# Layer 1 in the order of every fourth token, layer-0 entries turned by DMA, and a work list with shorter latencies: a four-layer graph network on one core

## The chip, the cores and the metric

The kernel runs on one core of a Trainium2 chip. The core has five engines with a queue each: TensorE (PE, matmul; its weight loads are shown as PEld), VectorE (DVE), ScalarE (ACT), GpSimd (POOL) and SyncE (SP), which here only issues DMAs. Each engine takes its instructions strictly in the order in which they stand in its queue and waits on semaphores for what the others produce. The metric is the device time of one execution in microseconds (us). Before the change it is 1746.38 us, the median of three runs (1745.01 to 1746.55).

## The reference

A batch of 32 graphs of 512 tokens with 128 features goes through four layers that share one adjacency matrix of zeros and ones. Each layer adds its result to x, after a layer norm and a relu:

```python
h = jnp.maximum(_layernorm(x, axis=-1), 0.0)
x = x + layer(h, adj, ...)
```

Layer 0 is an attention-like layer: `x_h = elu(h @ Wi + bi)`, two scores per token from `We`, `e = sigmoid(a_tgt[:, :, None] + a_src[:, None, :] + be)` times a mask made from the adjacency, then `agg = e @ x_h`, `self_part = x_h * sum(e, axis=-1)`, and two more products (`Wn` with an elu, `Wm`). Layer 1 is a gated recurrent unit of five steps:

```python
m_in = m_out = jnp.einsum('nm,bmd->bnd', adj, h)
av = jnp.concatenate([m_in, m_out], axis=-1)
u3 = h @ u3_w.T + u3_b
z = sigmoid(av @ w3_w.T + w3_b + u3); r = sigmoid(av @ w4_w.T + w4_b + u3)
hv = tanh(av @ w5_w.T + w5_b + (r * h @ u5_w.T + u5_b))
h = (1.0 - z) * h + z * hv
```

Layer 2 is `adj @ (h @ weight) + bias`. Layer 3 is a sum over powers zero to three of the adjacency, each with its own weight.

## The kernel before

A graph's tensor is one tile of 128 partitions by 512 f32 (256 KB). It is held in one of two ways: tokens on partitions (four chunks of 128 tokens side by side), or turned, with the features on partitions and 512 tokens along the row. Work goes in groups of four graphs (`G = 4`), eight groups. The tokens-on-partitions form is what the adjacency products take as the stationary operand, and what layer norm and the final sums need; the gate products need the turned form.

The kernel does not write its instructions in the order of the mathematics. It first lists operations: `op(engine, us, due, emit, reads, writes, ...)` records an engine, a duration, a due time and the values read and written. `Plan.order` (line 98) then plays the list through: at each moment it gives each engine that is free the ready operation with the earliest due time, provided that buffers are free (`slots`, line 223: 36 of kind f in SBUF, 8 PSUM banks of kind b, and so on). An operation's result counts as known `result` us after its end: the class constant `RESULT` (line 45) or a value of its own for DMAs. The outcome fixes the order of every engine's queue. Durations and due times are numbers written in the code; they change nothing but this order.

`begin(b)` (line 560) sets the due time of graph b: 14 us apart for the first ones (`FIRST_PACE`, line 217), 56 us apart later (`PACE`), so that at any time several graphs are in flight in different layers.

An adjacency entry that TensorE's fast f32r format cannot hold would need an exact f32 path. The kernel counts such entries (L424, L431, L436), branches once (L812 and L813, with everything up to a planned 30 us before the branch) and runs one of two lists. With zeros and ones it is the list with `A_r`, the f32r adjacency, where a token operand is split into a high and a low f32r part (`parts`, L672 on ScalarE and L675 on VectorE) and each adjacency product is eight passes (L686). The f32 products with the weights are all made by `product` (L357); each shows in the profile as two instructions.

- **Layer 0, entry.** `copied(transposed(h))`: four 128x128 transposes on TensorE (L329) into PSUM, a ScalarE copy (L352), then the product with Wi.
- **Layer 0, scores.** L469 makes messages and two scores per token; L476 puts the scores into `ends`, one column per chunk. One score is needed as a row on all partitions. For the first four graphs TensorE spreads it (`spread`, L493). For the others `gather` (L488) writes the four columns to DRAM as a row of 512 elements, and a second DMA (L502) reads it back to all 128 partitions.
- **Layer 0, sums.** GpSimd adds the four tiles of e (L516, three additions per graph) and one product with ones sums over partitions (L357 `ones` for the first four graphs; L533, L534 and L539 in f32r for the others).
- **Layer 1.** Its first turned h comes from TensorE like layer 0's. A step has the products u3, adjacency, w4, w3, w5 and u5, two VectorE additions (L704), three tanh (L362) and four more VectorE operations (L711, L721, L723, L725). Then `turned` (L337) brings the new h back to tokens on partitions without TensorE: VectorE transposes 32x32 blocks, reading every fourth token of a row, a DMA writes the result to DRAM (L340, m<-f) and a second one reads it back in pieces of 512 bytes, rearranged (L342, f<-m).
- **Layers 2 and 3.** L743; and L760 with L769.

SP issues all DMAs in one queue. A DMA that reads what another wrote waits in that queue until the other has landed.

Of the kernel before, what the change touches and what calls it, by code (L numbers as in the profile page):

```python
# [11 lines left out]
F32R = mybir.dt.float32r  # L12
# [4 lines left out]
P = 128  # L17
# [21 lines left out]
class Plan:  # L39
# [5 lines left out]
    RESULT = {"PE": 0.5, "ACT": 0.5, "DVE": 0.5, "POOL": 0.6, "SP": 2.5}  # L45
# [51 lines left out]

    def order(self, end=None):
# [9 lines left out]
        for i, o in enumerate(left):  # L108
            index[o] = i
            o.waits = sum(not b.begun for b in o.before)  # L110
            o.ready = max([0.0, *(b.known for b in o.before if b.begun)])
            if not o.waits:
                heapq.heappush(coming[o.eng], (o.ready, i, o))
                events.append(o.ready)
# [16 lines left out]
        while events:  # L131
# [3 lines left out]
            for e in self.until:  # L135
# [33 lines left out]
                for a in o.after:  # L169
                    if a in index:  # L170
                        a.waits -= 1
                        a.ready = max(a.ready, o.known)
# [8 lines left out]
def tile_four_graph_layers(  # L181
# [30 lines left out]
    G = 4  # L212
# [4 lines left out]
    PACE, FIRST_PACE, LAST_PACE = 56.0, 14.0, 30.0  # L217
# [3 lines left out]
    T_VEC, T_COPY, T_ACT = 0.61, 0.5, 0.6  # L221

    slots = {"x": 6, "f": 36, "q": 4, "s": 8, "d": 4, "m": 8, "b": 8}
# [8 lines left out]
    def buffers(pool, kind, n, shape, dt=F32):  # L232
# [7 lines left out]
        "d": buffers(dram, "d", slots["d"], [1, N]),  # L240
# [92 lines left out]
    def turned(src, due):  # L333


        blocks, moved, t = Val("f"), Val("m"), Val("f")
        op("DVE", 1.03, due, lambda: nc.vector.transpose(  # L337
            at(blocks).rearrange("p (q c f) -> p q c f", c=NC, f=32),
            at(src).rearrange("p (c i q) -> p q c i", c=NC, q=4)), [src], [blocks])
        op("SP", 1.0, due, lambda: nc.sync.dma_start(at(moved), at(blocks)),  # L340
           [blocks], [moved], result=4.0)
        op("SP", 1.0, due, lambda: nc.sync.dma_start(  # L342
            at(t).rearrange("p (b e) -> p b e", e=P),
            at(moved).rearrange("(b i) (q e) -> (i q) b e", i=32, e=P)), [moved], [t], result=6.0)
# [10 lines left out]
    def product(w, src, due, dst=None, start=True, stop=True):  # L355
        dst = dst or Val("b")
        op("PE", T_MM, due, lambda: nc.tensor.matmul(  # L357
            at(dst), at(w), at(src), start=start, stop=stop), [src, w], [dst])
# [50 lines left out]
    A_r, mask = const("A_r", [P, NC, N], F32R), const("mask", [P, NC, N])  # L409
    inexact = const("inexact", [1, 1], I32)  # L410
    n_odd = const("n_odd", [P, NC])
    for jc in range(NC):
        pt, z, odd = Val("b"), Val("f"), Val("f")
        def turn(jc=jc, pt=pt):
# [9 lines left out]
        op("DVE", 0.7, jc, lambda jc=jc, pt=pt, odd=odd: nc.vector.scalar_tensor_tensor(  # L424
            at(odd), at(A_r)[:, jc, :].bitcast(F32), 1.0, at(pt),
            op0=ALU.mult, op1=ALU.not_equal, accum_out=at(n_odd)[:, jc : jc + 1]),
            [A_r, pt], [odd, n_odd])
    p_odd = Val("b")
# [6 lines left out]
    op("PE", 0.3, 8, count, [n_odd, ones], [p_odd])  # L435
    op("DVE", 0.2, 8, lambda: nc.vector.tensor_copy(at(inexact), at(p_odd)[:1, :1]),  # L436
# [18 lines left out]
    def layer0(b, h, due):  # L455
        KEEP = 12
        hT = copied(transposed(h, due), due)
        d = due + 6
        xhT = elu(product(Wi_sb, hT, d), bi_sb, bi_half, d, KEEP)
# [25 lines left out]
        row, tgt = Val("d"), Val("f")  # L485
        def gather():
            with nc.allow_non_contiguous_dma(reason="a column of chunks becomes a row"):
                nc.sync.dma_start(  # L488
                    at(row).rearrange("o (c p) -> p (o c)", c=NC), at(ends)[:, NC : 2 * NC]
                )  # L490
# [9 lines left out]
        else:  # L500
            op("SP", 0.6, due + 10, gather, [ends], [row], result=11.0)
            op("SP", 0.6, due + 14, lambda: nc.sync.dma_start(  # L502
                at(tgt), at(row).to_broadcast([P, N])), [row], [tgt], keep=KEEP, result=7.0)
        es = []
        for jc in range(NC):
            e = Val("f")
            op("ACT", T_ACT, d, lambda e=e, jc=jc: nc.scalar.activation(
                at(e), at(tgt), AF.Tanh, bias=at(ends)[:, jc : jc + 1]), [tgt, ends], [e],
# [5 lines left out]
        sums = [Val("f"), Val("f")]  # L514
        def add(dst, a, c):
            op("POOL", 1.4, d, lambda: nc.gpsimd.tensor_tensor(  # L516
                at(dst), at(a), at(c), op=ALU.add), [a, c], [dst])
# [334 lines left out]
```

## Time and profile before

| | |
|---|---|
| median of three runs | 1746.38 us |
| the profiled execution | 1748.12 us |
| its span, first to last instruction | 1746.3 us |
| mean granted TensorE clock | 0.994 |
| DMA: moved, mean share of 16 engines | 112 MB, 24% |

Some groups of instructions, by line and tile:

| line, engine | what | count | mean ns | busy us |
|---|---|---|---|---|
| L337 DVE | transpose of 32x32 blocks, layer 1 | 160 | 1105 | 176.5 |
| L704 DVE | addition of u to a gate | 320 | 679 | 213.6 |
| L510 DVE | (tanh + 1) times mask, layer 0 | 128 | 900 | 107.8 |
| L516 POOL | sums of e, layer 0 | 96 | 1608 | 154.1 |
| L352 ACT | copies of PSUM to SBUF | 448 | 588 | 256.5 |
| L329 PE | transposes with the identity | 384 | 277 | 57.6 |

A row of the profile's groups gives busy time and the mean duration of one. Durations of matmuls overlap (a transpose is shown as 277 ns, though four follow each other in 0.44 us), so TensorE's work is better counted from how far long runs reach in the chain of waits. VectorE's instructions overlap a little too: a 128x512 elementwise one is shown as about 680 ns, and the next begins 600 ns after it.

The busy time by stretch, in us:

| stretch | PE | DVE | ACT | POOL | clock |
|---|---|---|---|---|---|
| 0-50 | 28.92 | 33.52 | 32.91 | 23.33 | 0.93 |
| 50-250 | 196.41 | 186.66 | 144.94 | 57.03 | 1.00 |
| 250-1450 | 1179.32 | 1051.69 | 805.69 | 290.17 | 0.99 |
| 1450-1700 | 249.17 | 194.38 | 145.15 | 29.23 | 1.00 |
| 1700-1746.3 | 41.66 | 13.02 | 6.47 | 0.00 | 0.98 |

### The profile page before, as it was taken

The page shows a single profiled execution, that of the slowest core. Times are in us where ns is not written, and L with a number is a line of the kernel's source. Part 1 is how long each engine was busy: PE and PEld are TensorE (multiplying, and loading weights), DVE is VectorE, ACT ScalarE, POOL GpSimd, SP SyncE. Part 2 cuts the span into 40 slices and gives each one's busy share as a digit, 9 for nine tenths or more (in the row PEclk, how much of TensorE's full clock was granted, in tenths as well). Part 3 has the DMA queues.
Part 4 walks back from the last instruction along what each step waited for, and adds up shares of the span by engine and source line. Part 5 has one row for each costly group of instructions (what it writes and reads, how often), then busy time and mean ns, then how long its engine had stood idle before and what let it go on. Part 6 is the DMA issues. An engine that isn't in the chain of part 4 may idle for free.

```text
span 1746.3 us, 21006 instructions
## 1 busy us (share of the span) xinstructions
PE 1695.5 (97%) x6829; PEld 1098.0 (63%) x6829; DVE 1479.3 (85%) x3213; ACT 1135.2 (65%) x2155; POOL 399.8 (23%) x312
## 2 busy tenths in 40 slices
PE   5899999999999999999999999999999999999998
PEld 3555555566666666665666666666666656656797
DVE  6899999999898887888888898888899879878752
ACT  6767765778666666665765667666768656655451
POOL 4521210332222211222212221122232212001110
PEclk9999999999999999999999999999999999999999
DMA  4022322322222222223221221222322131221201
GB/s 109 7 53 75 85 73 73 81 52 85 52 58 61 79 67 46 74 75 55 67 55 60 79 61 61 67 52 81 67 67 55 50 84 61 73 72 58 76 13 48
DMA packets 164534, 112.07 MB, mean 64 GB/s; under 512 B 23232, under 2 KB 139840, under 8 KB 164416
## 3 DMA queue, kind: packets, MB, share of 16 engines
q1 hardware_dynamic: 164416, 110.65, 23.9%
q8 instruction: 55, 0.90, 0.3%
q14 instruction: 63, 0.52, 0.2%
HBM read 60.23 MB, written 50.39 MB: 63 GB/s over the span
## 4 chain that ended last, share of the span: by engine, by line
PE 76%; DVE 13%; DMA 4%; ACT 3%; issue 2%; SPq 0%; DVEq 0%; ACTq 0%
PE b L357 33%; PE b L686 17%; PE b L769 9%; PE b L760 6%; DMA f<-m 4%; PE b L525 4%; PE b L552 3%; DVE f L510 2%; PE b L329 2%; DVE f L704 2%; PE b L743 2%; PE b L469 1%; DVE f L337 1%; DVE f L723 1%; DVE r L675 1%
## 5 line engine op out<-in xcount | busy, mean ns | idle before, releaser
L686 PE MATMUL b<-A_r,r 128*128 128x512 f32 x1536 | 427.6, 421 | 4.3 <-DVE r L675 4.2
L352 ACT COPY f<-b 128x512 f32<-128x512 f32 x448 | 256.5, 588 | 210.6 <-PE b L686 119.2
L686 PEld LDWEIGHTS b<-A_r,r 128*128 128x128 f32 x1536 | 287.2, 189 | 109.6 <-issue 38.9
L391 POOL TENSOR_TENSOR s<-s,nhalf 128x4 f32<-128x4 f32 x128 | 156.2, 1221 | 735.9 <-DVE s L389 707.8
L769 PE MATMUL b<-r,A_r 128*128 128x512 f32 x768 | 306.3, 499 | 0.0
L704 DVE TENSOR_TENSOR f<-f,b 128x512 f32<-128x512 f32 x320 | 213.6, 679 | 56.5 <-PE b L357 54.0
L399 ACT ACTIVATE f<-x,s 128x128 f32<-128x128 f32 x512 | 209.9, 488 | 22.3 <-DVE s L394 22.2
L769 PEld LDWEIGHTS b<-r,A_r 128*128 128x128 f32 x768 | 140.6, 189 | 102.6 <-issue 91.5
L516 POOL TENSOR_TENSOR f<-f,f 128x512 f32<-128x512 f32 x96 | 154.1, 1608 | 207.4 <-DVE f L510 131.1
L362 ACT ACTIVATE f<-f,b4w 128x512 f32<-128x512 f32 x160 | 115.8, 724 | 127.3 <-DVE f L704 126.6
L337 DVE STREAM_TRANSPOSE f<-f 128x512 f32<-128x512 f32 x160 | 176.5, 1105 | 0.3
L675 DVE TENSOR_TENSOR r<-f,r 128x512 fp32r<-128x512 f32 x192 | 141.3, 739 | 37.1 <-ACT r L672 37.0
L357 PE MATMUL b<-f,u5T 128*128 128x512 f32 x320 | 163.2, 595 | 8.7 <-DVE f L711 8.7
L357 PE MATMUL b<-f,w4T 128*128 128x512 f32 x320 | 165.2, 599 | 4.1 <-ACT f L352 4.0
L357 PE MATMUL b<-f,w3T 128*128 128x512 f32 x320 | 163.8, 594 | 0.0
L357 PE MATMUL b<-f,w5T 128*128 128x512 f32 x320 | 163.2, 595 | 0.0
L357 PE MATMUL b<-f,u3T 128*128 128x512 f32 x320 | 162.7, 592 | 0.0
L721 DVE TENSOR_TENSOR f<-f,f 128x512 f32<-128x512 f32 x160 | 121.5, 761 | 39.3 <-ACT f L362 39.1
L760 PEld LDWEIGHTS b<-V,f 128*128 128x128 f32 x1024 | 131.7, 191 | 31.1 <-issue 25.1
L362 ACT ACTIVATE f<-b,b5w 128x512 f32<-128x512 f32 x160 | 109.7, 688 | 60.4 <-PE b L357 60.2
L362 ACT ACTIVATE f<-f,b3w 128x512 f32<-128x512 f32 x160 | 115.0, 721 | 50.8 <-DVE f L704 50.5
L525 PE MATMUL b<-f,f 128*128 128x512 f32 x256 | 130.9, 596 | 3.2 <-issue 3.0
(95 smaller groups left out, 2489.9 us busy)
## 6 DMA issues: line engine op xcount, KB each, us to landing
m<-f SPq DMA_DIRECT2D x160, 256.0 KB, 2.0
f<-m SPq DMA_DIRECT2D x160, 256.0 KB, 2.8
x<-in_x_dram SPq DMA_DIRECT2D x32, 256.0 KB, 4.5
out_dram<-x SPq DMA_DIRECT2D x32, 256.0 KB, 2.4
f<-d SPq DMA_DIRECT2D x28, 256.0 KB, 4.1
f<-in_adj_dram SPq DMA_DIRECT2D x4, 256.0 KB, 4.6
f<-in_L_gnn_weight_dram SPq DMA_DIRECT2D x2, 224.0 KB, 2.6
d<-s SPq DMA_DIRECT2D x28, 2.0 KB, 9.1
```

What stands on the lines that cost most here:

```text
L337: op("DVE", 1.03, due, lambda: nc.vector.transpose(at(blocks).rearrange("p (q c f) -> p q c f", c=NC, f=32), at(src).rearrange("p (c i q) ...
L352: op("ACT", us, due, lambda: nc.scalar.copy(at(t), at(src)), [src], [t])
L357: op("PE", T_MM, due, lambda: nc.tensor.matmul(at(dst), at(w), at(src), start=start, stop=stop), [src, w], [dst])
L362: op("ACT", us, due, lambda: nc.scalar.activation(at(dst), at(src), AF.Tanh, bias=at(bias), scale=scale), [src, bias], [dst])
L391: op("POOL", 1.2, due, lambda: nc.gpsimd.tensor_tensor(stat(SCALE), stat(VAR), at(neg_half), op=ALU.pow), [s, neg_half], [s])
L399: nc.scalar.activation(at(h)[:, ts(c, P)], at(X[b])[:, c, :], AF.Relu, bias=stat(SHIFT)[:, c : c + 1], scale=stat(SCALE)[:, c : c + 1],)
L525: op("PE", T_MM, d, lambda jc=jc: nc.tensor.matmul(at(pn), at(msg)[:, ts(jc, P)], at(es[jc]), start=jc == 0, stop=False), [msg, es[jc]], [pn])
L675: op("DVE", T_VEC, due, lambda: nc.vector.tensor_tensor(part(lo), whole(), part(hi).bitcast(F32), op=ALU.subtract), [src, hi], [lo], two=two)
L686: nc.tensor.matmul(at(pa), at(part)[:, ts(jc, P)], at(adjT)[:, jc, :], start=jc == n == 0, stop=jc == NC - 1 and n == PARTS - 1,)
L704: op("DVE", T_VEC, d, lambda: nc.vector.tensor_tensor(at(s), at(u), at(pg), op=ALU.add), [u, pg], [s])
L760: nc.tensor.matmul(at(pz)[:, ts(i, D)], at(hT[i])[:, ts(ic, P)], at(V[k]), start=i == 0, stop=last and i == G - 1,)
L769: nc.tensor.matmul(at(pz), at(adjT)[:, jc, ts(ic, P)], at(part), start=False, stop=jc == NC - 1 and n == PARTS - 1,)
```

## The change

- **Layer 1 runs with its turned tiles in another token order.** In a chunk of 128 tokens, the 32 tokens 0, 4, 8, ... come first, then 1, 5, 9, ..., and so on. The copy into the first turned h makes this order (line 753 of the changed kernel), and layer 1's adjacency products take their columns from `A_fours`, a copy of the adjacency with its columns in the same order, made once by four ScalarE copies. `turned` now reads 32 elements in a row per block.
- **Layer 0 of graphs 4 to 31 gets its turned h by DMA**: `turned_back`, the same three operations as `turned` in the other direction, in place of the TensorE transposes and the copy. Its columns come out in blocks; the product with Wi reads them through a view with four dimensions.
- **The row of scores** goes to DRAM as 128 rows of 128 bytes: a VectorE transpose `flip` of the score columns, each repeated eight times, then one DMA; the read back takes the four rows of each quarter that are needed. The tile stays in blocks, and the tanh reads it through a view.
- **The first four graphs' sums** of e are four products with ones on TensorE; GpSimd's additions remain for the others, later due.
- **The list**: smaller `RESULT` values, no or a smaller delay between operations of the same engine (`known`), 0.45 us per DMA issue, 2.6 and 3.6 us for DMA results, `FIRST_PACE` 10 instead of 14, layer 1 of the first four graphs due 0.75 instead of 1.2 paces after layer 0, the count of inexact entries due later, five x buffers instead of six, and one free r buffer kept by `parts`.

```diff
-    RESULT = {"PE": 0.5, "ACT": 0.5, "DVE": 0.5, "POOL": 0.6, "SP": 2.5}
+    RESULT = {"PE": 0.25, "ACT": 0.2, "DVE": 0.2, "POOL": 0.2, "SP": 2.5}
...
+    def known(self, o, to):
+
+        own = {"PE": 0.0, "ACT": 0.13, "DVE": 0.13}
+        return o.known - o.result + own[o.eng] if to.eng == o.eng in own else o.known
...
-                        a.ready = max(a.ready, o.known)
+                        a.ready = max(a.ready, self.known(o, a))
...
-    PACE, FIRST_PACE, LAST_PACE = 56.0, 14.0, 30.0
+    PACE, FIRST_PACE, LAST_PACE = 56.0, 10.0, 30.0
...
-    slots = {"x": 6, "f": 36, "q": 4, "s": 8, "d": 4, "m": 8, "b": 8}
+    slots = {"x": 5, "f": 36, "q": 4, "s": 8, "d": 4, "m": 8, "b": 8}
...
     def turned(src, due):
...
+        op("DVE", 0.63, due, lambda: nc.vector.transpose(
+            at(blocks).rearrange("p (q c f) -> p q c f", c=NC, f=32),
+            at(src).rearrange("p (c q i) -> p q c i", c=NC, q=4)), [src], [blocks])
+        op("SP", T_DMA, due, lambda: nc.sync.dma_start(at(moved), at(blocks)),
+           [blocks], [moved], result=2.6)
+        op("SP", T_DMA, due, lambda: nc.sync.dma_start(
+            at(t).rearrange("p (b e) -> p b e", e=P),
+            at(moved).rearrange("(b i) (q e) -> (i q) b e", i=32, e=P)), [moved], [t], result=3.6)
+        return t
+
+    def turned_back(src, due):
+
         blocks, moved, t = Val("f"), Val("m"), Val("f")
         op("DVE", 1.03, due, lambda: nc.vector.transpose(
-            at(blocks).rearrange("p (q c f) -> p q c f", c=NC, f=32),
-            at(src).rearrange("p (c i q) -> p q c i", c=NC, q=4)), [src], [blocks])
-        op("SP", 1.0, due, lambda: nc.sync.dma_start(at(moved), at(blocks)),
-           [blocks], [moved], result=4.0)
...
+            at(blocks).rearrange("p (b c i) -> p b c i", c=NC, i=32),
+            at(src).rearrange("p (c f b) -> p b c f", c=NC, b=4)), [src], [blocks])
...
+    for jc in range(NC):
+        op("ACT", 0.52, 30, lambda jc=jc: nc.scalar.copy(
+            at(A_fours)[:, jc, :].rearrange("p (c q i) -> p c q i", c=NC, q=4),
+            at(A_r)[:, jc, :].rearrange("p (c i q) -> p c q i", c=NC, q=4)), [A_r], [A_fours])
...
-        hT = copied(transposed(h, due), due)
+        if b < G:
+            hT = copied(transposed(h, due), due)
+        else:
+            hT = turned_back(h, due)
+            due += 6
         d = due + 6
-        xhT = elu(product(Wi_sb, hT, d), bi_sb, bi_half, d, KEEP)
+        xhT = elu(product(Wi_sb, hT, d, blocks=b >= G), bi_sb, bi_half, d, KEEP)
...
+        def turn():
+            nc.vector.transpose(
+                at(flip)[:, :32].rearrange("p (k c) -> p k c", c=NC),
+                at(ends)[:, None, NC : 2 * NC].to_broadcast([P, 32 // NC, NC]))
         def gather():
-            with nc.allow_non_contiguous_dma(reason="a column of chunks becomes a row"):
-                nc.sync.dma_start(
-                    at(row).rearrange("o (c p) -> p (o c)", c=NC), at(ends)[:, NC : 2 * NC]
-                )
+            nc.sync.dma_start(at(row), at(flip)[:, :32])
+        def read():
+            rows = at(row).rearrange("(q k) i -> q (k i)", k=32)[:, :P]
+            nc.sync.dma_start(
+                at(tgt).rearrange("p (q e) -> p q e", e=P), rows[None].to_broadcast([P, 4, P]))
...
         if b < G:
-            ps = product(ones, sums[0], d)
+            ps = Val("b")
+            for jc in range(NC):
+                product(ones, es[jc], d, ps, start=jc == 0, stop=jc == NC - 1)
         else:
...
-            h = copied(transposed(h, due), due)
+            pt, h = transposed(h, due), Val("f")
+            op("ACT", T_COPY, due, lambda h=h, pt=pt: nc.scalar.copy(
+                at(h).rearrange("p (c q i) -> p c q i", c=NC, q=4), at(pt).rearrange("p (c i q) -> p c q i", c=NC, q=4)), [pt], [h])
...
-                m = copied(times_adj(tok, d), d)
+                m = copied(times_adj(tok, d, fours=True), d)
...
-                t = begin(b) + (2.0 if G <= b < B - G - 1 else 1.2) * PACE
+                t = begin(b) + (0.75 if b < G else 2.0 if b < B - G - 1 else 1.2) * PACE
```

## The prediction

> **What bounds the kernel now.** I read the shares of busy time first, then the busy time by slice, then I counted TensorE's work, then looked for the places where TensorE stands.
>
> ```profile
> span 1746.3 us, 21006 instructions
> PE 1695.5 (97%) x6829; PEld 1098.0 (63%) x6829; DVE 1479.3 (85%) x3213; ACT 1135.2 (65%) x2155; POOL 399.8 (23%) x312
> ...
> PE   5899999999999999999999999999999999999998
> ```
>
> TensorE is busy nearly everywhere, but matmul ends are modelled, so 97% does not say how much could be saved. I therefore count. The chain of waits gives the pace of long runs:
>
> ```profile
> 1599.16 8.58 PE b L357 x20
> 1691.38 5.36 PE b L760 x48
> 941.19 0.44 PE b L329 x4
> ```
>
> That is 0.429 us for an f32 128x512 instruction (two make one product, 0.858), 0.112 for a 128-wide one, 0.11 for a transpose (four are 0.44). The same view has 1.85 us for eight adjacency passes of L686 (0.231) and 6.36 for 28 of L769 (0.227). Times the counts of the groups: 1992 f32 instructions (5 x 320 gate ones, 256 of L525, 64 + 64 + 8 of Wi, Wn, ones) 854.6; 1536 of L686 354.8; 768 of L769 and 56 of L539 187.9; 2048 narrow ones (L760, L552, L743, L469) 228.8; 421 transposes 46.3. Sum **1672 us**, so the span holds about 74 us in which TensorE has nothing to do or runs at a lower clock. Doing the same count in stretches, the loss is 27.7 us in 0-50 (22.6 of it before 30), 4.8 in 50-250, 33.0 in 250-1450, 1.6 in 1450-1700 and 4.6 in the tail. The change can take instructions off TensorE, or these losses.
>
> The middle's losses come in lumps; three 50-us stretches alone lose 4.4, 5.6 and 4.1. Around one of them, first SP's DMA issues in order of time, then the chain, then TensorE's instructions, then one window (its length, busy PE, PEld, DVE, ACT, POOL, the granted clock, DMA):
>
> ```profile
> 792.54 0.36 SPq L488 DMA_DIRECT2D d<-s  x1
> 793.07 0.39 SPq L342 DMA_DIRECT2D f<-m  x1
> ```
>
> ```profile
> 793.07 11.55 DMA f<-m
> ```
>
> ```profile
> 806.38 2.08 PE L357 MATMUL b<-f,w4T 128*128 128x512 f32 x2 [2.15 <-ACT f L352]
> ```
>
> ```profile
> 807.00:808.00 1.00, 1.00 (x2) 0.34 (x1) 0.32 (x1) 1.00 (x4) 0.00 (x0) 0.50 0.04 14
> ```
>
> A write d<-s (one column of scores) is issued, and the f<-m right behind it lands after 11.55 us instead of its usual 2.8. ScalarE's queue stands on it (L672), so VectorE's and TensorE's do: 2.15 us of nothing, and then a clock of 0.50. The chain shows six such f<-m (304, 356, 518, 687, 793, 1417 us), each right behind a d<-s; those of 304, 793 and 1417 reach TensorE and are the three lumps.
>
> ```profile
> m<-f SPq DMA_DIRECT2D x160, 256.0 KB, 2.0
> f<-m SPq DMA_DIRECT2D x160, 256.0 KB, 2.8
> ...
> d<-s SPq DMA_DIRECT2D x28, 2.0 KB, 9.1
> ```
>
> The 2 KB of d<-s go as 512 pieces of 4 bytes and take 9.1 us, longer than 256 KB in 128 rows.
>
> **The change, part by part.**
>
> *Entries of layer 0 (graphs 4 to 31).* Four transposes per graph leave TensorE: 28 x 0.44 = **-12.3 us** where it is the bound; a ScalarE copy of 0.59 each goes too (off the path, 65% busy). In their place stand a VectorE transpose with the stride of today's L337, which takes 1.02 us from issue to issue, and an m/f pair of DMAs: 1.02 + 2.0 + 2.8 plus two issues of 0.35, some 6.5 us, before Wi. The list gives 6 us more for it, and three or four graphs in flight stand on TensorE's queue meanwhile: cost nothing; uncovered, it would be up to 6.5 us a graph. A rule speaks against this edit: the Trainium skill (VectorE: DVE Perf Modes, "Rules for kernel authors") says to use TensorE for a 128x128 transpose if a PSUM destination is acceptable, and its "The three transpose paths" warns of plain DMAs with strides. By the rule the 12.3 us stay in the sum (1729 below). The rows say otherwise here: 512-byte pieces land in 2.8 us, and the engine that is relieved is the one that is full. I take the row. Wi then reads its operand in 128-byte runs; no row shows that, between 0 and a doubling (28 x 0.858 = 24 us); I take 0, as an f32 product takes 0.858 us for 512 columns and so reads slowly.
>
> *Rows of layer 0.* d<-s becomes a small VectorE transpose (0.1-0.2 us, like the 0.2 of L476) and a DMA of 128 rows of 128 bytes. Its landing lies between 2.0 (m<-f, also 128 rows) and 9.1 (the present one). By number of pieces it is nearest to m<-f, so I take about 2. Then an f<-m behind it has nothing to wait for. What a lump costs: the Trainium skill (TensorE: Matmul & The Clock Gate, "Why this matters for your kernels") puts the loss of clock at idle gaps over about 3 us; by that the three stalls cost their gaps alone, 3 x 2.1 = 6.3. Here gaps of 2.1 us are followed by some 3 us at 0.50, so the measured 4.4 + 5.6 + 4.1 = **-14.1 us** stands. f<-d (4.1) stays 256 KB, in 512-byte pieces.
>
> *Token order in layer 1.* L337 (160 times) reads 32 elements in a row instead of every fourth. Between today's 1.02 and the 0.60 of every elementwise 128x512 row I take 0.60: 160 x 0.42 = -67 us of VectorE, against +28 x 1.02 for the new transposes and 28 small ones (+4): -34 us, from 85% busy to 83%. In 50-250 it is 93% busy (186.66 of 200). A_fours costs four ScalarE copies, about 2.4 us once, off the path; L686's moving operand stays contiguous, so 0.231 stays. The 32 copies that reorder h read PSUM with a stride: 0.59 up to twice that, on ScalarE, hidden. The x slots go from 6 to 5: a group lives some 800 us of the list's 224 per group, under four slots.
>
> *First four graphs.* The three POOL adds per graph (1.3-1.8 us each, in series, L516) go and TensorE does four "ones" products instead of one: 12 x 0.858 = **+10.3 us**. In graph 0 the product of ones starts at 37.97 today although its L510 are done at 30.9. Together with the 12.3: TensorE's work falls by 2.0 to **1670**.
>
> *The head.* Before 30 us it waits for the adjacency (first matmul at 6.3), for VectorE (busy without a break from 9.8 to 20) and for 3 us of branch: the same instructions stand before the branch, so its 22 us stay. After it, in the order in which the changed kernel's instructions stand on each engine, TensorE has 28 us of work up to the first adjacency pass of layer 1 and VectorE 20 us, for which about 29 us are there (31 to 60); today the first pass comes at 73.7, and 30-60 lose 6.1 us. Layer 1, which asks 6.1 us of TensorE per step for 5 of VectorE, comes earlier (0.75 instead of 1.2 paces). I take 2 us of loss for 31-60 and 2 for 60-250 instead of 6.1 and 3.3, and 22 before: 26 for 32.5, **-6.5 us**. Ends: -9.5 (1 us lost after 31) and 0.
>
> *The list's latencies.* Results count as known after 0.2-0.25 us instead of 0.5, DMAs after 2.6 and 3.6 instead of 4 and 6 (medians 2.0 and 2.8). Nothing is added or removed; order changes. The remaining 33.0 - 14.1 = 18.9 us of the middle are waits for VectorE such as the one at 931 (L721 and L711 1.68 us each beside POOL's L516). Less VectorE work and later-due POOL adds shorten it; a tighter order has less slack. Bounds: all 18.9 gone, or 19 more. I take a third off, **-6 us**.
>
> Sum against the profiled 1746.3: -2.0 - 14.1 - 6.5 - 6 = **1717.7 us**. The profiled execution took 1748.1 in all, 1.7 over the median 1746.4, so a median of the runs near 1717.
>
> **Rivals.** *(1) The middle keeps its stalls.* The lumps at 310, 800 and 1430 go, but the tighter order opens others, since slack that covered VectorE's delays is gone. For it: VectorE is still 83% busy and in order; against it: three of the four clock losses have one cause. Only -2.0 and -6.5 remain, with up to a few us of the rest: 1737. *(2) The middle becomes clean:* all 33.0 go and the head gains 9.5: 1746.3 - 2 - 33 - 9.5 = 1702. *(3) Slower: SP's queue.* SP issues in order and stands at each f<-m until its m<-f has landed (272.5 us in all, 124 waits). 28 more pairs go through it, before which and behind which layer 1's pairs stand; a late pair would stop ScalarE's queue as at 805, at 2.1 us and 1.7 of clock, 3.9 each. It decides from (28.7 + 3.5) / 3.9 = 8 such stalls; at one in every other graph, 14, it is 1717.7 + 55 = 1772. Against it: DMAs are 24% busy, SP's pairs take some 3 us each and 7 are asked per 56 us.
>
> **How the numbers follow.** Likeliest case 60% (1706-1728, by its own ends); rival 1 22% (1728-1743); rival 2 9%; rival 3 9%. No change to be told from noise is within 0.2%, 3.5 us. Faster: 60 + 9 + nearly all of rival 1, 88%; same 3%; slower 9%. The range 1700 to 1740 leaves out rival 3 and a part of rival 1.
>
> **What would show it.** d<-s landing near 2 us and no f<-m over 6; L337's successor near 0.6 instead of 1.02 from issue to issue; granted clock of 1.00 in nearly all of 250-1450; 272 instead of 384 records of L329's transposes; first adjacency pass near 60 us. I am wrong if TensorE's pace changes (Wi above 0.858, adjacency passes above 0.231), if d<-s still takes over 6 us, or if waits of TensorE for ScalarE behind f<-m multiply.

## The result, and the profile after

| | before | after |
|---|---|---|
| median of the runs | 1746.47 us (1745.01 to 1747.39, n = 4) | 1720.19 us (1719.12 to 1721.13, n = 4) |
| profiled execution, its span | 1746.3 us | 1717.3 us |

The ratio is 0.985, with an interval of 0.9833 to 0.9867. The change makes the kernel faster by 26 us; the forecast was 1717, within 1700 to 1740. The total is therefore right to 3 us (the profiled span, against which the sum was made, to 0.4 us). Whether its terms are right is another matter, and most of what follows is about them.

The page after: engines, then TensorE by slice with its clock.

```profile
span 1717.3 us, 20992 instructions
...
PE 1687.2 (98%) x6741; PEld 1088.6 (63%) x6741; DVE 1421.1 (83%) x3269; ACT 1130.1 (66%) x2131; POOL 374.8 (22%) x300
...
PE   6999999999999999999999999999999999999998
...
PEclk8999999999999999999999999999999999999999
```

TensorE's busy time fell by only 8.3 us while the span fell by 29.0, so most of the gain is time in which TensorE stood or was throttled. The same page's DMA issues (count, KB each, median us to landing), those that answer to the ones before:

```profile
m<-f SPq DMA_DIRECT2D x188, 256.0 KB, 2.0
f<-m SPq DMA_DIRECT2D x188, 256.0 KB, 2.8
...
f<-d SPq DMA_DIRECT2D x28, 256.0 KB, 5.1
...
d<-s SPq DMA_DIRECT2D x28, 16.0 KB, 1.4
```

The score row lands in 1.4 us instead of 9.1 and its read back takes 5.1 instead of 4.1. The pairs m<-f, f<-m land as before, although there are 28 more. The chain of waits, which had six f<-m of some 11 us, has none.

Groups by line and tile, for the single prices:

```profile
L382 PE MATMUL b<-f,Wi_sb 128*128 128x512 f32 x64 | 33.9, 611 | 0.8 <-ACT f L371 0.8
...
L334 PE MATMUL b<-ident,f 128*128 128x128 f32 x272 | 40.6, 278 | 7.0 <-ACT f L424 7.0
...
L343 DVE STREAM_TRANSPOSE f<-f 128x512 f32<-128x512 f32 x160 | 112.1, 703 | 0.5
...
L356 DVE STREAM_TRANSPOSE f<-f 128x512 f32<-128x512 f32 x28 | 31.4, 1123 | 0.8 <-ACT f L424 0.7
...
L753 ACT COPY f<-b 128x512 f32<-128x512 f32 x32 | 19.0, 595 | 3.1 <-PE b L334 3.1
...
L456 ACT CAST A_fours<-A_r 128x512 fp32r<-128x512 f32 x4 | 4.3, 1140 | 0.0
```

The transposes left are the predicted 272. Layer 1's DVE transpose (L343) is shown as 703 ns, as an elementwise one is, where the strided one was 1105; the new one of layer 0 (L356) has that older price. The reordering copy from PSUM costs what any copy does (595 against 585 of L371). Wi with its operand in blocks is shown as 611 ns (594 before the change); over 64 instructions that is 1 us. Only the copies to A_fours surprise: 1140 ns each, once.

Four windows (length; busy PE, PEld, DVE, ACT, POOL with counts; granted clock; DMA share; GB/s) and the first adjacency pass of layer 1 in the chain (start, length, what):

```profile
0.00:30.00 30.00, 14.68 (x51) 9.51 (x52) 15.83 (x63) 20.65 (x37) 8.95 (x17) 0.75 0.38 109
30.00:60.00 30.00, 29.93 (x113) 16.47 (x112) 20.73 (x62) 23.58 (x54) 9.99 (x13) 0.97 0.26 77
60.00:250.00 190.00, 190.00 (x663) 111.03 (x662) 168.17 (x359) 136.38 (x251) 40.12 (x34) 1.00 0.24 74
250.00:1450.00 1200.00, 1190.37 (x4710) 761.38 (x4708) 1044.05 (x2398) 816.60 (x1547) 288.55 (x215) 1.00 0.25 77
```

```profile
62.24 1.84 PE b L742 x8
```

The same of the kernel before, its window of 30 to 60 us and its first adjacency pass:

```profile
30.00:60.00 30.00, 24.82 (x104) 14.03 (x104) 28.44 (x63) 21.53 (x48) 19.98 (x18) 1.00 0.18 50
```

```profile
73.67 2.11 PE b L686 x8
```

Layer 1 begins at 62.2 us (73.7 before), and from 60 to 250 TensorE is never idle. To compare, I count TensorE's instructions of each stretch at the paces of the prediction and subtract them from the stretch's length. What is left is the loss, in us. An instruction that crosses a boundary is counted on both sides of it, so that a loss is up to about 1 us too small and can fall below zero; the last 70 us, some 5 us of loss in every kernel, are left out. The work in all is the count of the whole kernel at these paces, not a measured time.

| kernel | work in all | 0-30 | 30-60 | 60-250 | 250-1450 | on to last 70 us |
|---|---|---|---|---|---|---|
| before | 1672.2 | 22.6 | 6.1 | 3.3 | 33.0 | 1.5 |
| after | 1670.2 | 23.0 | 0.9 | -0.7 | 16.4 | -0.5 |

So the span's 29.0 us are, to 0.1, 2.0 of work, 8.8 up to 250 us, 16.6 in the middle and 2.0 behind it, less 0.5 in the tail. The middle still loses 16.4 us, now at a full clock.

### The profile page after: what moved, and what is told of

Same layout as the page of the kernel before. It is cut to its first block, busy times and chain, and to the rows that moved or that the text cites. A ratio compares the mean times of both kernels' runs of the same rounds, so it can differ in the third digit from the quotient of the medians.

```text
span 1717.3 us, 20992 instructions
## 1 busy us (share of the span) xinstructions
PE 1687.2 (98%) x6741; PEld 1088.6 (63%) x6741; DVE 1421.1 (83%) x3269; ACT 1130.1 (66%) x2131; POOL 374.8 (22%) x300
## 4 chain that ended last, share of the span: by engine, by line
PE 84%; DVE 8%; ACT 4%; DMA 3%; issue 1%; SPq 0%; POOL 0%; DVEq 0%; ACTq 0%; POOLq 0%
PE b L382 38%; PE b L742 17%; PE b L827 10%; PE b L818 6%; PE b L566 4%; PE b L602 3%; DVE f L558 3%; DMA f<-d 2%; PE b L334 2%; PE b L504 1%; PE b L801 1%; ACT f L424 1%; DVE f L762 1%; PE b L589 1%; ACT f L387 1%
## 5 line engine op out<-in xcount | busy, mean ns | idle before, releaser
L742 PE MATMUL b<-A_fours,r 128*128 128x512 f32 x1280 | 376.0, 436 | 0.0
L371 ACT COPY f<-b 128x512 f32<-128x512 f32 x388 | 224.8, 585 | 159.8 <-PE b L742 107.0
L742 PEld LDWEIGHTS b<-A_fours,r 128*128 128x128 f32 x1280 | 239.1, 188 | 104.4 <-issue 58.1
L827 PE MATMUL b<-r,A_r 128*128 128x512 f32 x768 | 223.8, 428 | 0.0
L577 POOL TENSOR_TENSOR f<-f,f 128x512 f32<-128x512 f32 x84 | 125.2, 1491 | 261.6 <-DVE f L558 185.4
L779 DVE TENSOR_TENSOR f<-f,f 128x512 f32<-128x512 f32 x160 | 115.6, 724 | 75.4 <-ACT f L387 74.9
L726 DVE TENSOR_TENSOR r<-f,r 128x512 fp32r<-128x512 f32 x192 | 133.5, 697 | 14.1 <-ACT r L722 13.8
L818 PE MATMUL b<-V,f 128*128 128x128 f32 x1024 | 132.7, 275 | 0.0
L566 PE MATMUL b<-f,f 128*128 128x512 f32 x256 | 121.9, 604 | 2.8 <-DVE f L558 2.7
```

The costliest lines, as they stand in the source:

```text
L371: op("ACT", us, due, lambda: nc.scalar.copy(at(t), at(src)), [src], [t])
L566: op("PE", T_MM, d, lambda jc=jc: nc.tensor.matmul(at(pn), at(msg)[:, ts(jc, P)], at(es[jc]), start=jc == 0, stop=False), [msg, es[jc]], [pn])
L577: op("POOL", 1.4, d - 10, lambda: nc.gpsimd.tensor_tensor(at(dst), at(a), at(c), op=ALU.add), [a, c], [dst])
L726: op("DVE", T_VEC, due, lambda: nc.vector.tensor_tensor(part(lo), whole(), part(hi).bitcast(F32), op=ALU.subtract), [src, hi], [lo], two=two)
L742: nc.tensor.matmul(at(pa), at(part)[:, ts(jc, P)], view(at(columns)[:, jc, :]), start=jc == n == 0, stop=jc == NC - 1 and n == PARTS - 1,)
L818: nc.tensor.matmul(at(pz)[:, ts(i, D)], at(hT[i])[:, ts(ic, P)], at(V[k]), start=i == 0, stop=last and i == G - 1,)
```

## The experiments

Twelve kernels ran, in three lots: e1 to e4 and later e9 to e12 on one chip, e5 to e8 on another. The kernel before took 1758.58, 1760.14 and 1759.70 us in the three lots (1746.47 on the chip of the result above), the changed kernel itself (e9) 1722.37. Ratios are to the kernel before on the same chip; unless said otherwise, microseconds are compared with e9. The losses of all, counted as above:

| kernel | median us | ratio [interval] | work | 0-30 | 30-60 | 60-250 | 250-1450 |
|---|---|---|---|---|---|---|---|
| e1_rows4 | 1889.71 | 1.0758 [1.0734, 1.0783] | 1670.2 | 23.0 | 1.3 | 13.8 | 154.3 |
| e2_before_rows128 | 1733.66 | 0.9861 [0.9844, 0.9877] | 1672.2 | 23.0 | 6.1 | 9.9 | 9.7 |
| e3_pe_turn | 1738.81 | 0.9894 [0.9873, 0.9916] | 1682.5 | 23.0 | 1.0 | 1.7 | 20.1 |
| e4_natural | 1719.10 | 0.9779 [0.9763, 0.9796] | 1670.2 | 23.0 | 0.5 | -0.1 | 15.8 |
| e5_pool_sums | 1723.96 | 0.9800 [0.9784, 0.9817] | 1659.9 | 23.5 | 6.5 | 5.2 | 20.6 |
| e6_one_graph | 1724.38 | 0.9802 [0.9785, 0.9818] | 1661.3 | 23.0 | 6.5 | 5.6 | 18.7 |
| e7_old_latencies | 1714.15 | 0.9741 [0.9724, 0.9757] | 1670.2 | 23.0 | 3.5 | 1.4 | 7.7 |
| e8_old_head | 1725.93 | 0.9808 [0.9792, 0.9824] | 1670.2 | 23.5 | 2.6 | 0.5 | 20.4 |
| e9_same_chip | 1722.37 | 0.9791 [0.9775, 0.9807] | 1670.2 | 23.0 | 1.3 | -0.7 | 19.3 |
| e10_rows4_slack | 1762.64 | 1.0021 [1.0009, 1.0033] | 1670.2 | 23.0 | 2.6 | 9.2 | 45.4 |
| e11_mixed | 1711.37 | 0.9727 [0.9714, 0.9741] | 1670.2 | 23.5 | 1.3 | -0.5 | 9.3 |
| e12_mixed_dma | 1712.29 | 0.9731 [0.9717, 0.9745] | 1670.2 | 23.5 | 1.8 | -0.5 | 9.9 |

Behind 1450 us, e1 loses another 16.7 us and e10 2.9, the others nothing.

**e1_rows4: the change with the old row of 4-byte pieces.**

```diff
-        "d": buffers(dram, "d", slots["d"], [P, 32]),
+        "d": buffers(dram, "d", slots["d"], [1, N]),
...
-            nc.sync.dma_start(at(row), at(flip)[:, :32])
+                    at(row).rearrange("o (c p) -> p (o c)", c=NC), at(ends)[:, NC : 2 * NC]
...
-            op("DVE", 0.1, d, turn, [ends], [flip])
-            op("SP", T_DMA, d, gather, [flip], [row], result=2.6)
-            op("SP", T_DMA, d, read, [row], [tgt], keep=KEEP, result=3.6)
+            op("SP", T_DMA, d - 10, gather, [ends], [row], result=11.0)
+            op("SP", T_DMA, d - 6, read, [row], [tgt], keep=KEEP, result=7.0)
```

> The changed kernel with the row of scores written in 512 pieces of 4 bytes again (due times and delays in the list as before the change). Theory (the pieces block the DMA behind them): a d<-s takes about 9 us again, some f<-m land after 10 us or more, TensorE's loss in the middle (16.4 us in 250-1450 now) grows by 8 to 15: 1728 to 1735 us. Rival (the lumps had gone because VectorE has less to do and the list is different): 1717 to 1723 us, whatever the d<-s take.

Measured: 1889.71 us, 167 above the change and 131 above the kernel before. Both expectations are far off. SP's DMA issues in order of time at one place (start, length, what), then the chain there, then a window and ScalarE's waits for f<-m in 250-1450 (us in all, times, longest), all of e1:

```profile
860.70 0.37 SPq L529 DMA_DIRECT2D d<-s  x1
862.54 0.33 SPq L359 DMA_DIRECT2D m<-f  x1
862.96 0.39 SPq L348 DMA_DIRECT2D f<-m  x1
873.41 0.36 SPq L361 DMA_DIRECT2D f<-m  x1
```

```profile
862.96 11.19 DMA f<-m
874.15 0.02 issue
874.17 0.63 ACT r L720
874.80 0.02 issue
874.83 0.69 DVE r L724
875.52 0.60 DVE f L781
876.12 0.61 DVE f L767
876.73 0.04 issue
876.78 2.07 PE b L382 x2
```

```profile
876.00:882.00 6.00, 5.22 (x12) 3.21 (x13) 5.12 (x16) 2.37 (x4) 1.39 (x1) 0.50 0.47 128
```

```profile
ACT r L720 <- DMA f<-m: 119.9, 21, 8.1
```

The f<-m issued 2.3 us after a d<-s takes 11.19 us. Of the f<-m whose landing the trace gives, 12 take more than 6 us, and each was issued 0.5 to 3.4 us after a d<-s. SP's queue stands: the second f<-m, issued only at 873.41, waits for its m<-f of 862.54, which itself sits behind the d<-s. In the chain, ScalarE's split (L720), then VectorE, then TensorE start only once the first has landed, and the two matmuls at 876.78 then take 2.07 us instead of 0.86, at a granted clock of 0.50. ScalarE waits for f<-m 33 times, 149.1 us in all, of them 21 in the middle. The middle loses 154.3 us: the changed list, with a pair of DMAs more per graph and little slack, stands at the late DMA which the old list mostly outwaited.

**e2_before_rows128: the kernel before with nothing new but the row** and its landing time in the list.

```diff
-        "d": buffers(dram, "d", slots["d"], [1, N]),
+        "d": buffers(dram, "d", slots["d"], [P, 32]),
...
-            op("SP", 0.6, due + 10, gather, [ends], [row], result=11.0)
-            op("SP", 0.6, due + 14, lambda: nc.sync.dma_start(
-                at(tgt), at(row).to_broadcast([P, N])), [row], [tgt], keep=KEEP, result=7.0)
+            op("DVE", 0.1, due + 10, turn, [ends], [flip])
+            op("SP", 0.6, due + 10, gather, [flip], [row], result=4.0)
+            op("SP", 0.6, due + 14, read, [row], [tgt], keep=KEEP, result=7.0)
```

> The kernel before with nothing changed but the row of scores: 128 rows of 128 bytes by way of a VectorE transpose, and 4 us instead of 11 in the list for its landing. Theory: d<-s lands in 1.4 to 2 us, no f<-m over 6 us, the three lumps go: 1746 - 14 = 1732 us (1728 to 1737). Rival (the lumps come from VectorE's load or the list): 1743 to 1749 us.

Measured: 1733.66 us. That is near the time expected, but from a higher start: it is 25 under the kernel before on the same chip, not 14. Its DMA issues:

```profile
f<-d SPq DMA_DIRECT2D x28, 256.0 KB, 5.1
...
d<-s SPq DMA_DIRECT2D x28, 16.0 KB, 1.4
```

The longest f<-m of this kernel takes 5.8 us (12.2 before), and the middle's loss is 9.7 us instead of 33.0, with VectorE's strided transposes still there. The two profiles come from different chips, and e2's is of its fastest run, 4.2 us under its median. So the old row cost the middle about 19 to 23 us, an estimate from these numbers, and not the 14 of the three lumps; 6.6 us come back between 60 and 250, and why was not followed. The 25 us hold for this chip. Here d<-s of 4-byte pieces lands in 10.8 to 10.9 us (e1, e10; 9.1 before, on the first chip) and the kernel before is 12 us slower, while the changed one is 2 us slower. If e2 moves as little as that, its worth on the first chip is about 1746.47 - 1733.66 = 13 us. It lies between 13 and 25; it was not run there.

**e3_pe_turn: TensorE transposes again for all graphs.**

```diff
-        if b < G:
-            hT = copied(transposed(h, due), due)
-        else:
-            hT = turned_back(h, due)
-            due += 6
+        hT = copied(transposed(h, due), due)
...
-        xhT = elu(product(Wi_sb, hT, d, blocks=b >= G), bi_sb, bi_half, d, KEEP)
+        xhT = elu(product(Wi_sb, hT, d), bi_sb, bi_half, d, KEEP)
```

> The changed kernel with layer 0's turned h from TensorE for all graphs again (112 more transposes, 28 more ScalarE copies, 28 fewer VectorE transposes and 56 fewer DMAs). Theory: TensorE's work is the bound, so +28 x 0.44 = +12.3 us, less a few us that VectorE's 29 us less give back: 1728 to 1733 us. Rival (TensorE has slack beside these, VectorE and the DMA queue set the time): 1716 to 1722 us.

Measured: 1738.81 us, 16.4 more than the change: the side of the theory that the transposes cost their work, and somewhat more. The group of transposes of e3:

```profile
L334 PE MATMUL b<-ident,f 128*128 128x128 f32 x384 | 56.4, 277 | 6.9 <-ACT f L424 6.9
```

112 instructions come back, at the old pace, so that the work rises by the 12.3 us that were counted. The remaining 4.1 us are 2.4 of loss between 60 and 250, 0.8 in the middle, and the spread of the runs (1736.46 to 1742.89). Moving the entry to VectorE and DMA is worth its whole price.

**e4_natural: natural token order in layer 1**, so that VectorE's transposes are strided again and A_fours is not used.

```diff
-        op("DVE", 0.63, due, lambda: nc.vector.transpose(
+        op("DVE", 1.03, due, lambda: nc.vector.transpose(
...
-            at(src).rearrange("p (c q i) -> p q c i", c=NC, q=4)), [src], [blocks])
+            at(src).rearrange("p (c i q) -> p q c i", c=NC, q=4)), [src], [blocks])
...
-                m = copied(times_adj(tok, d, fours=True), d)
+                m = copied(times_adj(tok, d), d)
```

> The changed kernel with layer 1's turned tiles in the natural token order: the 160 VectorE transposes read with a stride again (1.02 instead of about 0.6 us from issue to issue, +67 us of VectorE), A_r for all adjacency products. Theory (VectorE is not the bound, its load only makes some small waits): +3 to +8 us, 1723 to 1728. Rival 1 (VectorE bounds the middle): +15 us or more, over 1735. Rival 2 (it is hidden altogether): within 2 us of 1720.

Measured: 1719.10 us; the intervals of e4 and e9 overlap, so no cost shows: the rival that VectorE's time is hidden altogether. e4's engines and its transpose:

```profile
PE 1686.7 (98%) x6741; PEld 1088.1 (63%) x6741; DVE 1476.6 (86%) x3269; ACT 1125.1 (66%) x2131; POOL 382.9 (22%) x300
```

```profile
L343 DVE STREAM_TRANSPOSE f<-f 128x512 f32<-128x512 f32 x160 | 176.7, 1105 | 0.7
```

VectorE is busy for 55.5 us more than after the change, and the time is no longer. The new token order, the part that the change is named for, buys nothing here; with the slacker list of e11 it was not tried.

**e5_pool_sums and e6_one_graph: the head's sums of e on GpSimd again,** for all four first graphs, or for three of them.

```diff
+        sums = [Val("f"), Val("f")]
...
-            ps = Val("b")
-            for jc in range(NC):
-                product(ones, es[jc], d, ps, start=jc == 0, stop=jc == NC - 1)
+            ps = product(ones, sums[0], d)
```

In e6 only the condition changes:

```diff
-        if b < G:
+        if b < 1:
```

> The changed kernel with GpSimd's additions and a single product with ones for the first four graphs, as before the change. TensorE's work falls by 12 x 0.858 = 10.3 us. Theory: after 31 us TensorE's queue is full except for what graph 0 holds up, so most of the 10.3 is kept for graphs 1 to 3 (7.7) and graph 0 gives some back: 1712 to 1720 us. Rival (the additions' latency holds the head, as it did before): 1722 to 1730 us.

> The changed kernel with the four products with ones for graph 0 alone; graphs 1 to 3 take GpSimd's additions and the split in f32r of the later graphs. TensorE's work falls by 3 x (3.43 - 0.46) = 8.9 us. Theory: nothing of graphs 1 to 3 is waited for, so 1711 to 1714 us. Rival (their latency counts too): 1718 us or more.

Measured: 1723.96 and 1724.38 us, ratios 0.9800 and 0.9802 against 0.9791 of e9: no difference that can be told. These are the times that the rivals forecast. Two windows of e5, and, of the waits of its weight loads in 30-250 that have a named cause, the longest (waiting line, for what; us in all, times, longest):

```profile
30.00:60.00 30.00, 25.05 (x103) 13.86 (x102) 24.48 (x61) 23.31 (x51) 19.21 (x18) 1.00 0.19 50
60.00:250.00 190.00, 186.51 (x644) 106.89 (x643) 171.50 (x361) 137.05 (x253) 47.90 (x40) 1.00 0.25 78
```

```profile
PEld b L382 <- DVE f L590: 5.7, 5, 2.5
PEld b L566 <- DVE f L558: 5.5, 11, 1.1
PEld b L334 <- ACT f L424: 3.6, 3, 3.1
```

TensorE has 10.3 us less to do and stands 11.1 us more: 6.5 + 5.2 up to 250 us against 1.3 - 0.7. GpSimd is busy for 19.2 of the 30 us instead of 10. The ones products of the change fill time in which TensorE would otherwise stand; in time they buy nothing that can be told. To sum graph 0 alone with them frees nothing either: e6 stands as long as e5. The rivals' cause, the latency of GpSimd's additions, is not shown: TensorE waits for VectorE and ScalarE, and between 30 and 80 us the chain of waits has no piece of GpSimd in either kernel. Whether the additions act through the order of the list was not followed.

**e7_old_latencies: the change with the old delays of results,** on all engines but SP's DMAs.

```diff
-    RESULT = {"PE": 0.25, "ACT": 0.2, "DVE": 0.2, "POOL": 0.2, "SP": 2.5}
+    RESULT = {"PE": 0.5, "ACT": 0.5, "DVE": 0.5, "POOL": 0.6, "SP": 2.5}
...
-        own = {"PE": 0.0, "ACT": 0.13, "DVE": 0.13}
-        return o.known - o.result + own[o.eng] if to.eng == o.eng in own else o.known
+        return o.known
```

> The changed kernel with the list's former delays of results (0.5 us on all engines, none of its own for the same engine; the DMAs' new ones stay). Only the order of the queues changes. Theory (the order's slack is of little weight): within 4 us of 1720, 1717 to 1724. Rival (the smaller delays made the middle clean): the 16.6 us gained in 250-1450 come back, 1732 to 1738.

Measured: 1714.15 us, some 8 us faster than the change (0.9741 against 0.9791; the intervals do not meet). Both expectations fall: neither had a gain like it. The waits of TensorE's weight loads in 250-1450 (waiting line, for what; us in all, times, longest), first after the change, then e7:

```profile
PEld b L382 <- DVE f L769: 19.0, 29, 1.8
PEld b L566 <- DVE f L558: 16.3, 32, 1.9
```

```profile
PEld b L381 <- DVE f L768: 5.6, 8, 1.4
...
PEld b L565 <- DVE f L557: 1.7, 7, 0.2
```

The lines of e7 are one lower: the first row is u5 waiting for r times h, the second the aggregation waiting for the masked scores. 35 us of such waits become 7. They are not the loss itself, since a weight load can wait beside a running matmul, but the middle's loss goes with them, from 16.4 (19.3 in e9) to 7.7. In the head it is the other way round: 30-250 lose 4.9 us in e7 and 0.6 in e9. So the small delays gain 4 us in the head and cost about 10 in the middle.

**e8_old_head: the old pacing of the first graphs.**

```diff
-    PACE, FIRST_PACE, LAST_PACE = 56.0, 10.0, 30.0
+    PACE, FIRST_PACE, LAST_PACE = 56.0, 14.0, 30.0
...
-                t = begin(b) + (0.75 if b < G else 2.0 if b < B - G - 1 else 1.2) * PACE
+                t = begin(b) + (2.0 if G <= b < B - G - 1 else 1.2) * PACE
```

> The changed kernel with the first graphs 14 us apart and layer 1 of the first four due after 1.2 paces, as before the change. Theory (layer 1's work early fills TensorE in 30-250 us): the loss there, 0.2 us now, rises by 4 to 8 us: 1724 to 1728. Rival (the head's gain comes from the sums on TensorE): within 2 us of 1720.

Measured: 1725.93 us, as expected in kind, with the size at the edge of what can be told. The head loses 2.5 us more between 30 and 250 (3.1 against 0.6) and 0.5 before 30; the whole differs by about 3.5 us, though the ratio's interval still meets that of e9. The new pacing gains perhaps 3 us, which is not clear of the spread.

**e9_same_chip: the changed kernel itself,** for comparison.

> The changed kernel itself, unchanged, on the chip of the next three. It has no lumps, so it should not move with the chip: 1717 to 1722 us, while the kernel before may lie anywhere from 1745 to 1760.

Measured: 1722.37 us (1721.69 to 1724.19).

**e10_rows4_slack: e1 with e7's old delays,** and DMA results known after 4.0 and 6.0 us as before the change; the edits are those of e1 and e7, and

```diff
-           [blocks], [moved], result=2.6)
+           [blocks], [moved], result=4.0)
...
-            at(moved).rearrange("(b i) (q e) -> (i q) b e", i=32, e=P)), [moved], [t], result=3.6)
+            at(moved).rearrange("(b i) (q e) -> (i q) b e", i=32, e=P)), [moved], [t], result=6.0)
```

> The changed kernel with the row of scores in 4-byte pieces again, as in the first experiment (169 us more), but with the list's former delays on all engines (0.5 us) and former DMA results (4 and 6 us). Theory (a list with slack hides what the pieces hold up, a list without it passes each on to TensorE): 1730 to 1750 us, with as many f<-m over 6 us as in the first experiment. Rival (28 more round trips through the DMA queue meet the pieces more often, whatever the list says): over 1800 us.

Measured: 1762.64 us, 127 less than e1, nearer to the theory's range than to its rival's, and level with the kernel before to 0.2% (ratio 1.0021). ScalarE's wait for f<-m, 149.1 us in e1:

```profile
ACT r L719 <- DMA f<-m: 60.0, 20, 6.8
```

The late DMAs are still there (11 of the f<-m whose landing the trace gives take over 6 us, against 12 in e1), but less waits for them. Slack in the list is what made the slow row bearable; how much of it is the engines' delays and how much the DMA results, this run does not part. It follows, too, that without the new row the rest of the change, here with the old delays, is worth nothing on this chip: the row gains 25 us on its own (e2), about 48 on top of the rest with the old delays (e10's 1762.64 against e7's ratio, 0.9741 x 1759.70 = 1714.1) and 167 on top of the change (e1 against e9).

**e11_mixed: small delays for what is due before 150 us, the old ones later.**

```diff
+    LATER = {"PE": 0.5, "ACT": 0.5, "DVE": 0.5, "POOL": 0.6, "SP": 2.5}
+    HEAD = 150.0
...
-        o = Op(eng, us, self.RESULT[eng] if result is None else result, emit, two, keep)
+        delays = self.RESULT if due < self.HEAD else self.LATER
+        o = Op(eng, us, delays[eng] if result is None else result, emit, two, keep)
+        o.head = due < self.HEAD
...
-        return o.known - o.result + own[o.eng] if to.eng == o.eng in own else o.known
+        return o.known - o.result + own[o.eng] if o.head and to.eng == o.eng in own else o.known
```

> The changed kernel with its own small delays for operations due before 150 us in the list, and the former 0.5 us after that. Theory (small delays fill the head, slack keeps the middle clean): loss of 0.2 us in 30-250 as in the changed kernel and 7.7 in 250-1450 as with the former delays, 1714.2 - 4.7 = 1709 us (1706 to 1712). Rival (the two gains exclude each other, or are chance of one order): 1713 to 1720.

Measured: **1711.37 us**, 11 under the change on the same chip, below both kernels, and in the range expected. Two windows of e11, and the waits of its weight loads in 250-1450:

```profile
30.00:60.00 30.00, 29.08 (x112) 16.05 (x111) 21.37 (x62) 23.75 (x55) 10.01 (x12) 0.99 0.28 80
...
250.00:1450.00 1200.00, 1194.03 (x4739) 767.70 (x4738) 1045.22 (x2412) 825.14 (x1563) 286.59 (x216) 1.00 0.25 77
```

```profile
PEld b L386 <- DVE f L773: 7.4, 10, 3.1
PEld b L746 <- DVE r L730: 6.4, 7, 2.1
PEld b L570 <- DVE f L562: 2.6, 8, 1.0
```

The head keeps what the small delays gain (losses of 1.3 and -0.5), and the middle loses 9.3 us, near e7's 7.7. The first and the last of these rows are those that had 35 us in the change.

**e12_mixed_dma: e11 with DMA results known after 4.0 and 6.0 us,** the edit shown at e10, in both directions of turning.

> The same with the former DMA results of 4 and 6 us for the two turns as well. Theory: m<-f and f<-m land in 2.0 and 2.8 us and 2.6 and 3.6 cover that, so the extra slack changes little: within 4 us of the mixed kernel. Rival (DMA slack is what keeps the middle clean): 4 us or more below it; or the later entries of layer 0 cost: 4 us or more above it.

Measured: 1712.29 us, within 1 us of e11. With the new row, it does not matter whether the list counts the two turning DMAs near their measured medians or with twice the room. The middle's loss now stands in three kernels with the old delays after the head (7.7, 9.3 and 9.9 us in e7, e11, e12) and in six with the small ones (15.8 to 20.6 in the change and e3, e4, e5, e6, e8). That is not the chance of one order.

## Why the prediction was right, and where it was not

- **Work, -2.0: right.** The counts are those foreseen (272 transposes), and the paces hold: eight adjacency passes in 1.84 us, a transpose shown as 278 ns, Wi within 1 us in all. The transposes' 12.3 us come back in full when TensorE makes them again (e3). The rule that a transpose belongs on TensorE (the Trainium skill, VectorE: DVE Perf Modes, "Rules for kernel authors") would have cost e3's 16.4 us here: where TensorE is the bound, the row was the better guide. The ones products' +10.3 us, counted here as a plain cost, are paid back in the head.
- **Lumps, -14.1: right in mechanism, of uncertain size.** The row's write is the cause: with it and its landing time in the list changed and nothing else, no f<-m takes over 5.8 us any more (e2). In the middle it is worth some 19 to 23 us, so that part of the other 18.9 us, which I put down to VectorE, went with it; which waits these were was not followed. (A 50-us stretch is counted some 0.5 us short at its boundaries, so that the three lumps are nearer 15.6 and the rest nearer 17.) In the whole it is worth 13 to 25, by chip. The landing of 1.4 us lies under the lower bound of 2.0, for which m<-f with its 256 KB was no bound at all. As to the clock, gaps of 2.1 us before were followed by about 3 us at 0.50. The rule which I weighed against it, of gaps over about 3 us (the Trainium skill, TensorE: Matmul & The Clock Gate, "Why this matters for your kernels"), would have counted 6.3; the middle gained more than either.
- **Head, -6.5: right in sign and place, 2.3 too small.** 30-60 lose 0.9 and 60-250 nothing, where I took 2 and 2; before 30 us it is 23.0 (22 taken). (The 32.5 us from which I started are 32.0 by the stretches of the table.) But 8.8 us less loss is not 8.8 us gained: e5 and e6 show that the ones products fill 11.1 us of it and cost 10.3 of work, so that they buy no time that can be told. What remains are 4 us of small delays (e7) and perhaps 3 of pacing (e8), which may overlap.
- **"The list's latencies. ... I take a third off, -6 us": the step that failed.** It joined two things and had no row for the size of either. *VectorE's relief* is worth nothing in this list: its busy time fell by 58 us (34 were forecast), and e4 gives 55 back at no cost. *The small delays* cost the middle about 10 us (e7, e11) where I expected a gain. "A tighter order has less slack" stood in the text as the upper bound's reason, and was what happened. The middle as a whole gained 16.6 us where 14.1 + 6 = 20.1 were forecast: the row gave more than its term and the delays took some 10 back. The two errors nearly cancel, and the head's surplus of 2.3 and 2.0 behind 1450 us made up the rest. That the total came out so close is luck.
- **The rivals.** Rival 1 (other stalls open) is half true: the small delays did open waits, but on top of a middle that the row had cleared. Rival 2 (all of it gone) is what e11 comes near, with 9.3 us left. Rival 3 (SP's queue) did not come, since its cause went with the row; e1 is its picture: in the middle ScalarE waits 21 times and the loss is 138 us above the change's 16.4, 6.6 for each where I had counted 3.9.

Open: how exactly a small delay costs. The list places a consumer into TensorE's queue as soon as it believes the result known, so that one placed 0.2 us behind VectorE's L558 would stand at each late L558. The traces show two things that make it late: its own spread (shortest, median and longest ns), and ScalarE's tanh before it, which waits for the read back of the row. The first two lines are of the change, the third of e7:

```profile
L558 DVE SCALAR_TENSOR_TENSOR f<-f,mask x128: 647/688/1785, 25.5 to 1413.1; 128x512 f32<-128x512 f32 x128
```

```profile
ACT f L555 <- DMA f<-d: 12.2, 12, 1.9
```

```profile
ACT f L554 <- DMA f<-d: 12.2, 14, 2.4
```

Of the 24 L558 over 0.9 us, 23 go beside an addition of GpSimd (L577); 24 others do too and stay short, so what stretches them is not settled. And f<-d lands in 5.1 us where the list counts 3.6. In e7 ScalarE waits for it as long, but f<-d stands in the chain of waits three times there, against seven in the change and ten in e9. No run changed the spread of L558 or the 3.6 us of f<-d alone. Nor were the later due times of GpSimd's additions and the buffer counts taken back. Open, too, are the 9 to 10 us that the middle of the best kernel still loses, and why the kernel before is slower by 12 us on the other chips.

## What to carry to other kernels

Before an engine's relief is counted as a gain, look for the DMA behind which its queue stands: one transfer in 4-byte pieces held up those issued after it, and part of the waits that I had put down to a busy VectorE went with it. Delays in a hand-made order are slack against late results: in this kernel small ones paid where the pipeline fills, and room paid where it runs full. A forecast whose total is right proves little about its terms: here the small delays, part of a term of -6 us, cost the middle about 10, and reverting them for the later work alone gave the best kernel, 1711.37 us.

## What the runs showed of the hardware

- A DMA of 128 rows of 128 bytes (16 KB) lands in 1.4 us, sooner than one of 256 KB in 128 rows (2.0). The same scores as 512 pieces of 4 bytes took 9.1 us on one chip and 10.8 to 10.9 on another, and an f<-m issued 2.3 us behind one landed after 11.19 us (e1) instead of 2.9.
- Reading the row back as four pieces of 512 bytes per partition takes 5.1 us, against 3.9 to 4.2 for 2 KB (e1, e10). ScalarE waited for it 12 times, 12.2 us in all (after).
- A transpose of 32x32 blocks on VectorE, f32 128x512, is shown as 1105 ns when it reads every fourth element and 703 ns when it reads 32 in a row. On ScalarE a stride in PSUM cost nothing (595 against 585 ns), while the copy from SBUF to f32r with such a stride took 1140, against 620 without it (L722).
- VectorE's L558 takes a median of 688 ns, and some 1.75 us in 23 places, all beside an addition of GpSimd; 24 others beside one stayed short (after).
- After 2.15 us in which TensorE stood, the granted clock was 0.50 (before, at 807); after 4.78 us of it, 0.50 from 876 to 882 (e1).
